# Loading the index first, broadcasting coefficients by a matmul, halving the first parts, and adding W to one block by DMA

## The chip, the cores and the metric

The kernel runs on one core of a Trainium2 chip. TensorE multiplies matrices into PSUM; VectorE and ScalarE work element by element; GpSimd and SyncE here mostly issue DMAs. SyncE, ScalarE and GpSimd each have a DMA queue of their own, and all queues share the core's 16 DMA engines. The metric is the device time of one execution in microseconds (us), lower is better: 408.46 us is the median of three runs before the change.

## What is computed

Two layers follow each other on x, eight batches of 256 tokens by 1024. In the first layer each batch has its own integer mask of 1024 by 1024 and its own coefficient; in the second each batch picks one of eight weight matrices by an index.

```python
def _L0_cond_ref(hidden_states, W, b, coeff, mask):
    output = jnp.einsum('bsi,oi->bso', hidden_states, W) + b
    sign = (2 * mask - 1).astype(hidden_states.dtype)
    diff = jnp.einsum('bsi,bio->bso', hidden_states, sign)
    return output + diff * coeff[:, None, None]

def _L1_cond_ref(x, weight, adapter_ids):
    w = weight[adapter_ids]
    return jnp.einsum('bsi,boi->bso', x, w)

x = x + _L0_cond_ref(x, L0_cond_W, L0_cond_b, condB_coeff, mask_Bx4096x4096_ik1)
x = x + _L1_cond_ref(x, L1_cond_weight, itok_B_3_7)
```

For one batch the first layer is one product: x times (W transposed + coeff * (2 * mask - 1)). So each mask block is scaled on ScalarE to 2 * coeff * mask - coeff and W is added to it ("folded") before it is used as a weight.

## The kernel before

**Stages.** The very first stage is batch 0 of layer 0 (L285 on TensorE): eight row blocks k of mask and W, 128 rows each, are loaded in nine pieces, scaled on ScalarE (L271), folded on VectorE (L278) and multiplied. All other stages are pairs of a layer and a batch, in the order (1,0), (0,1), (0,2), (1,1), (0,3), (1,2) and so on up to (1,7). In this text they are stage 1, stage 2, stage 3 and so on; stage 1 uses L553 on TensorE, the later ones L563. The third batch (b = 2) of layer 0 is stage 3.

**A stage.** Each matrix of 1024 by 1024 is cut into four blocks "11", "12", "22", "21" of 512 by 512 (1 MB each, 8 KB in each of 128 partitions). Seven block products, p1 to p7 in the manner of Strassen and Winograd, stand for eight: p1, p5, p6, p2, p7, p3, p4 in this order on TensorE. The sums of weight blocks t1 to t4 (L515) and of input blocks s1 to s4 (L503) are made on VectorE, the products are added to the result on VectorE (L627), and two of them are copied out of PSUM by ScalarE on the way (L599: s after p1, u after p6; p7 waits for u, since it continues in the same PSUM bank). In layer 0, ScalarE scales each mask block (L476) and VectorE folds W into it (L490). The sum t1 is block 12 minus block 11; p5 needs s1 and t1, p1 needs block 11 itself, and s1 is a21 + a22.

**Results and residuals.** The residual of a batch is loaded by SyncE (L370), and the bias is added to it by a DMA with addition on GpSimd's queue (L380). Results of layer 0 are transposed on VectorE (L400) and moved into place by 32 small ScalarE operations (L414), which the first product of layer 1 for this batch waits for. Finished blocks are stored by GpSimd's queue (L653), 256 KB each, 2 KB in each partition.

**What sets the order.** Every engine has its own queue and works through it in order. The order is made when the kernel is built: each operation is a task with an engine, a length and a due time; plan() runs through them with a list of ready tasks for each engine, takes the most urgent one whose buffers are free, and the instructions are written in the order of the planned starts. Weight blocks live in eleven buffers ("w"). Changed lengths, or a task on another engine, can therefore reorder all that follows. At most eight loads are under way at once: SyncE issues a load only when the one eight places before it has landed.

**Around the change.** The coefficients come as a DMA that repeats one row in 128 partitions (L742); two VectorE operations make 2c and -c of it (L751, L752). The index of the second layer's weights (ids_sb, L756) and the bias column b_sb (L757) are issued on SyncE's queue when the last but two of the first stage's folds has been written down. SyncE reads the index into a register (L470) before the first weight load of stage 1 (L472); this read waits until the index has landed. Four evictions (L312) turn the first stage's PSUM banks into the input of stage 1. Eight matmuls on zeros (L750) run at the start.

Of the kernel before, what the change touches and what calls it, by code (L numbers as in the profile page):

```python
# [17 lines left out]
WBUFS = 11  # L18


PRODUCTS = (
    ("p1", "a11", "11"),
    ("p5", "s1", "t1"),
    ("p6", "s2", "t2"),
    ("p2", "a12", "21"),
    ("p7", "s3", "t3"),
    ("p3", "s4", "22"),
    ("p4", "a22", "t4"),
)

BANK = {"p1": "u", "p6": "u", "p7": "u", "p4": "u", "p5": "v", "p3": "v", "p2": "w"}
A_SLOT = {"a11": 0, "a12": 1, "a21": 2, "a22": 3, "s1": 4, "s2": 5, "s3": 2, "s4": 6}
# [9 lines left out]
}  # L42


PRODUCT, BLOCK, SMALL = 3.44, 2.30, 0.72
SCALE, COPY, SHUFFLE = 2.12, 0.65, 0.47
LOAD, STORE, LATENCY = 2.55, 0.65, 2.2


class Task:  # L50
# [20 lines left out]
def plan(tasks, room, may_take):  # L71
# [11 lines left out]
    for t in tasks:  # L83
        ready.setdefault(t.engine, [])
        if not waiting[t]:
            ready[t.engine].append(t)
    free_at = dict.fromkeys(ready, 0.0)
    left = {}
    events, now, done = [], 0.0, 0
    while done < len(tasks):  # L90
        for engine, queue in ready.items():
            if free_at[engine] > now + 1e-9:
# [34 lines left out]
def kernel(  # L127
# [58 lines left out]
    const = pools["const"]  # L186
    ids_sb = const.tile([1, B], I32, name="ids_sb")
    b_sb = const.tile([P, KC], F32, name="b_sb")
    c_sb = const.tile([P, B], F32, name="c_sb")
    c2_sb = const.tile([P, B], F32, name="c2_sb")  # L190
    cn_sb = const.tile([P, B], F32, name="cn_sb")
    warm = const.tile([P, 1], F32, name="warm")
    zeros = const.tile([P, H], BF16, name="zeros")
    w0_sb = const.tile([P, KC, 2, H], F32, name="w0_sb")
# [1 line left out]

    def block(q: str) -> int:
        return 2 * (int(q[0]) - 1) + int(q[1]) - 1

    w1_blocks = w1T.rearrange("n q p k o -> (n q) p k o")  # L200
    tasks: list[Task] = []
# [2 lines left out]
    def task(*args, **kw):  # L204
        tasks.append(Task(*args, **kw))
        return tasks[-1]
# [35 lines left out]
    first = {(j, h): Buffer("ps") for j in range(2) for h in range(2)}  # L242
    xb = Buffer("r")
    half = KH // 2
    pieces = [(0, ds(0, H)), (0, ds(H, H))] + [(k, ds(0, D)) for k in range(1, KC)]
    w0_rows = w0_sb.rearrange("p k j n -> p k (j n)")

    def x0_view():
# [7 lines left out]
    def load_x0(lo: int, hi: int, queue):  # L256
        queue.dma_start(out=x0_view()[:, lo:hi], in_=x0T[:, lo:hi])

    def load_first(n: int):
        k, cols = pieces[n]  # L260
        if m[k // 2].tile is None:
            take(m[k // 2])
        nc.sync.dma_start(out=m_view(k)[:, cols].bitcast(I32), in_=mask0[k][:, cols])  # L263
        nc.sync.dma_start(out=w0_rows[:, k, cols], in_=w0T[k][:, cols])  # L264
        if n in (1, 2, 4):
            load_x0(*{1: (1, 2), 2: (2, KH), 4: (KH, KC)}[n], nc.sync)

    def scale_first(n: int):
        k, cols = pieces[n]
        t = m_view(k)[:, cols]  # L270
        nc.scalar.activation(  # L271
            t, t.bitcast(I32), AF.Identity, bias=cn_sb[:, 0:1], scale=c2_sb[:, 0:1]
        )

    def fold_first(n: int):
        k, cols = pieces[n]
        t = m_view(k)[:, cols]
        v.tensor_tensor(t, t, w0_rows[:, k, cols], ALU.add)  # L278

    def mm_first(k: int, cols):  # L280
        for oc in range(cols.start // P, (cols.start + cols.size) // P):
# [35 lines left out]
        )  # L317

    at = 2.0
    folded: list[Task] = []  # L320
    for n, (k, cols) in enumerate(pieces):
        share = cols.size / D
        ld = task(
            "DMA",
            2.7 * share,
            lambda n=n: load_first(n),
            takes=[m[k // 2]] if n == 0 or (k % 2 == 0 and n > 1) else [],
            uses=[] if n == 0 or (k % 2 == 0 and n > 1) else [m[k // 2]],
            latency=2.0,
            latest=0.1 * n,  # L330
        )
        sc = task("ACT", 1.25 * share, lambda n=n: scale_first(n), after=[ld], uses=[m[k // 2]])
        fo = task("DVE", 1.25 * share, lambda n=n: fold_first(n), after=[sc], uses=[m[k // 2]])
        folded.append(fo)
        last_scale = sc
        if n == 0:
            tasks[0].takes = [x0] + list(tasks[0].takes)
            tasks[0].uses = [x0] + list(tasks[0].uses)
            x0.users += 1
# [90 lines left out]
    def stage(s: int):  # L430
# [49 lines left out]
        for q in BLOCKS:  # L480
            W[q] = Buffer("w")
            t = task("DMA", LOAD, lambda q=q: load(q), takes=[W[q]], latency=LATENCY)
            t.stage = s
            loads.append(t)
            if layer == 0:
                t = task("ACT", SCALE, lambda q=q: scale(q), after=[t], uses=[W[q]])
                t = task(
                    "DVE",
                    BLOCK,
                    lambda q=q: v.tensor_tensor(W[q].tile, W[q].tile, w0[q], ALU.add),  # L490
                    after=[t],
                    uses=[W[q]],
                )
            done[q] = t
        ready_r = load_r(b, begin) if layer == 0 else None

        def sum_of(what: str, after=()):
            left, op, right = SUMS[what]
            if what[0] == "s":
                done[what] = task(  # L500
                    "DVE",
                    SMALL,
                    lambda: v.tensor_tensor(part(what), part(left), part(right), op),  # L503
                    after=[*got, done.get(left), done.get(right), *after],
                    takes=[apart] if flipped and what == "s3" else [],
                    uses=[A],
                )
                return
            src = [W[left], W[right]]
            fresh = what in ("t2", "t3") or (what == "t1" and s == 1)  # L510
            W[what] = Buffer("w") if fresh else W[left]

            def emit():
                a, c = src[0].tile, src[1].tile
                v.tensor_tensor(take(W[what]) if fresh else W[what].tile, a, c, op)  # L515

            t = task(
                "DVE",
                BLOCK,
                emit,  # L520
                after=[done[left], done[right], *after],
                takes=[W[what]] if fresh else [],
                uses=src,
            )
            if fresh:
                t.stage = s
            done[what] = t

        sum_of("s1")
        sum_of("s2")  # L530
# [38 lines left out]
                    skip_group_check=True,  # L569
                )  # L570

        def add_product(n: int, after=()):
            nonlocal last_mm
            name, a, w = PRODUCTS[n]
            bank = BANK[name]
            opens = bank not in banks
            if opens:
                banks[bank] = Buffer("ps")
            r = banks[bank]
            needed = got if a[0] == "a" else []  # L580
            if flipped and a == "a11":
                needed = got[:2]
            mm[name] = last_mm = task(
                "PE",
                PRODUCT,
                lambda: product(name, a, w, r, opens),
                after=[last_mm, done[w], done.get(a), *needed, *after],
                takes=[r] if opens else [],
                uses=[A, W[w]] + ([] if opens else [r]) + ([apart] if flipped and a == "s3" else []),
                latest=begin + n * PRODUCT,  # L590
            )

        def keep(name: str, source: str):
# [65 lines left out]
                latency=3.0,  # L659
            )  # L660

        add_product(0)
        s1, s1_done = keep("s1", "p1")
        add_product(1)
        add("11", s1, ALU.add, s1_done)
        add_product(2, [s1_done])
        t = add("22", banks["v"], ALU.add, mm["p5"])
        u2, u2_done = keep("u2", "p6")
        add("12", u2, ALU.add, u2_done)
        add_product(3)  # L670
        sum_of("t4", [mm["p2"]])
        add("11", banks["w"], ALU.add, mm["p2"])
        finished("11")
        add_product(4, [u2_done])
        add_product(5, [t])
        t = add("22", banks["u"], ALU.add, mm["p7"])
        finished("22")
        if final:
            t = add("21", banks["u"], ALU.add, mm["p7"])
        add("12", banks["v"], ALU.add, mm["p3"])  # L680
        finished("12")
        if not final:
            add_product(6, [t])
            add("21", banks["u"], ALU.add, mm["p4"])
            finished("21")
        else:
# [52 lines left out]

    with tc.manual_schedule():  # L740
        take(x0)
        nc.scalar.dma_start(out=c_sb, in_=coeff.to_broadcast((P, B)))  # L742
        load_x0(0, 1, nc.scalar)
        v.memset(zeros, 0.0)
        v.memset(warm, 0.0)  # L745

        nc.scalar.activation(warm, warm, AF.Identity, bias=warm, scale=1.0)
        idle = pools["ps"].tile([P, H], F32, tag="ps", name="idle")
        for _ in range(8):
            nc.tensor.matmul(out=idle, lhsT=zeros[:, 0:P], rhs=zeros, start=True, stop=True)  # L750
        v.tensor_scalar(c2_sb, c_sb, 2.0, None, ALU.mult)  # L751
        v.tensor_scalar(cn_sb, c_sb, -1.0, None, ALU.mult)  # L752
        for n, t in enumerate(plan(tasks, room, may_take)):
            t.emit()
            if t is folded[-3]:
                nc.sync.dma_start(out=ids_sb, in_=ids)  # L756
                nc.sync.dma_start(out=b_sb, in_=biasT)  # L757
    if DUMP:
        for t in sorted(tasks, key=lambda t: t.start):
            print("PLAN %s %.2f %.2f %.2f" % (t.engine, t.start, t.end, t.latest))  # L760
# [55 lines left out]
```

## Time and profile before

| What | Value |
|---|---|
| Median of three runs | 408.46 us (408.2 to 408.93) |
| The profiled execution: its time, its span | 408.25 us, 406.5 us |
| Granted TensorE clock | 0.999 |
| ScalarE busy | 183.1 us (45%) |
| GpSimd busy | 25.9 us (6%) |
| HBM traffic | 94.38 MB read, 8.39 MB written |
| Fold of W into a 1 MB mask block on VectorE (L490) | 28 of 2281 ns |
| Sum of two weight blocks on VectorE (L515) | 60 of 2285 ns |
| Scaling of a 1 MB mask block on ScalarE (L476) | 28 of 2091 ns |
| Bias addition by DMA (L380), issue to landing | 7 of 7.8 to 16.4 us, median 9.9 |
| Store of a finished block (L653), issue to landing | 31 of 2.0 to 17.8 us, median 6.2 |

The span runs from the first to the last instruction in one profiled execution. "Busy" counts instructions on an engine; TensorE's matmuls are pipelined and each is recorded as two records in this program. A "wait" line names who waited, who ended the wait, and the time in total, how often, and the longest.

### The profile page before, as it was taken

The page shows a single profiled execution, that of the slowest core. Times are in us where ns is not written, and L with a number is a line of the kernel's source. Part 1 is how long each engine was busy: PE and PEld are TensorE (multiplying, and loading weights), DVE is VectorE, ACT ScalarE, POOL GpSimd, SP SyncE. Part 2 cuts the span into 40 slices and gives each one's busy share as a digit, 9 for nine tenths or more (in the row PEclk, how much of TensorE's full clock was granted, in tenths as well). Part 3 has the DMA queues.
Part 4 walks back from the last instruction along what each step waited for, and adds up shares of the span by engine and source line. Part 5 has one row for each costly group of instructions (what it writes and reads, how often), then busy time and mean ns, then how long its engine had stood idle before and what let it go on. Part 6 is the DMA issues. An engine that isn't in the chain of part 4 may idle for free.

```text
span 406.5 us, 3436 instructions
## 1 busy us (share of the span) xinstructions
PE 395.7 (97%) x1152; PEld 201.2 (49%) x1152; DVE 329.5 (81%) x300; ACT 183.1 (45%) x301; POOL 25.9 (6%) x42
## 2 busy tenths in 40 slices
PE   6997999999999999999999999999999999999996
PEld 3886996443444444444444444444444444444443
DVE  1345989899999979989989999799997989878142
ACT  4351642221991079422867445495117940283000
POOL 0000022001000210011100101002010010001101
PEclk9999999999999999999999999999999999999999
DMA  7979999998863869928697457987569582611102
GB/s 267 411 290 426 423 392 336 348 388 344 231 272 113 304 212 256 410 94 329 215 376 285 147 187 225 343 339 243 214 154 406 230 303 104 268 42 52 52 0 104
DMA packets 18804, 103.00 MB, mean 253 GB/s; under 512 B 2466, under 2 KB 2978, under 8 KB 9314
## 3 DMA queue, kind: packets, MB, share of 16 engines
q1 hardware_dynamic: 13970, 87.11, 54.7%
q0 software_dynamic: 4384, 15.47, 15.0%
q10 hardware_dynamic: 432, 0.20, 0.2%
q8 instruction: 9, 0.15, 0.1%
q14 instruction: 9, 0.07, 0.1%
HBM read 94.38 MB, written 8.39 MB: 253 GB/s over the span
## 4 chain that ended last, share of the span: by engine, by line
PE 82%; DMA 8%; DVE 4%; ACT 3%; issue 1%; SPq 1%; DVEq 0%; ACTq 0%
PE ps L563 77%; PE ps L553 5%; DMA w<-mask 4%; ACT a L414 3%; DMA ids_sb<-ids 2%; DMA w<-w1T 2%; DVE w L515 2%; DVE w L490 1%; DVE a L312 1%; DVE a L503 0%; DVE r L627 0%; SPq L264 0%; SPq L263 0%; SPq L470 0%; ACT u L599 0%
## 5 line engine op out<-in xcount | busy, mean ns | idle before, releaser
L563 PE MATMUL ps<-w,a 128*128 128x512 f32 (+1 forms) x792 | 337.2, 588 | 1.2 <-DVE a L503 0.7
L563 PEld LDWEIGHTS ps<-w,a 128*128 128x128 f32 x792 | 149.7, 190 | 188.6 <-issue 181.8
L515 DVE TENSOR_TENSOR w<-w,w 128x2048 f32<-128x2048 f32 x60 | 136.4, 2285 | 10.8 <-DMA w<-w1T 5.5
L414 ACT ACTIVATE a<-turn 32x256 f32<-32x256 f32 x224 | 92.7, 414 | 32.1 <-DVE turn L400 29.4
L476 ACT ACTIVATE w<-w,cn_sb,c_sb 128x2048 f32<-128x2048 int32 x28 | 58.2, 2091 | 32.6 <-DMA w<-mask 32.3
L627 DVE TENSOR_TENSOR r<-r,ps 128x512 f32<-128x512 f32 x73 | 49.5, 682 | 22.3 <-PE ps L563 21.6
L490 DVE TENSOR_TENSOR w<-w,w_sb 128x2048 f32<-128x2048 f32 x28 | 63.7, 2281 | 3.2 <-ACT w L476 3.2
L599 ACT ACTIVATE s<-ps 128x512 f32<-128x512 f32 x15 | 8.9, 594 | 85.4 <-PE ps L563 85.4
L503 DVE TENSOR_TENSOR a<-a 128x512 f32<-128x512 f32 x59 | 39.2, 680 | 0.1
L653 POOL DMA_DIRECT2D out<-r x31 | 17.5, 565 | 242.3 <-DVE r L627 239.4
L285 PE MATMUL ps<-a,w 128*128 128x256 f32 x128 | 29.4, 394 | 2.0 <-DVE w L278 2.0
L285 PEld LDWEIGHTS ps<-a,w 128*128 128x128 f32 x128 | 25.3, 199 | 6.6 <-DVE w L278 2.9
L599 ACT ACTIVATE u<-ps 128x512 f32<-128x512 f32 x15 | 9.0, 597 | 39.9 <-PE ps L563 39.2
L553 PE MATMUL ps<-a,w 128*128 128x128 f32 x192 | 22.3, 277 | 2.9 <-DVE a L312 2.2
L553 PEld LDWEIGHTS ps<-a,w 128*128 128x128 f32 x192 | 21.7, 192 | 3.6 <-DVE a L312 2.6
L278 DVE TENSOR_TENSOR w<-w,w_sb 128x1024 f32<-128x1024 f32 (+1 forms) x9 | 10.0, 1106 | 14.9 <-DMA w_sb<-w0T 9.4
L400 DVE STREAM_TRANSPOSE turn<-r 128x512 f32<-128x512 f32 x28 | 18.9, 695 | 0.1
L380 POOL DMA_DIRECT2D r<-bias x7 | 8.7, 1247 | 132.6 <-DMA r<-xR 132.6
L271 ACT ACTIVATE w<-w,cn_sb,c_sb 128x1024 f32<-128x1024 int32 (+1 forms) x9 | 10.3, 1145 | 15.1 <-DMA w<-mask 13.2
L627 DVE TENSOR_TENSOR r<-r,s 128x512 f32<-128x512 f32 x14 | 9.5, 681 | 8.1 <-ACT s L599 8.0
L627 DVE TENSOR_TENSOR r<-r,u 128x512 f32<-128x512 f32 x14 | 9.6, 688 | 6.8 <-ACT u L599 6.7
L750 PE MATMUL idle<-zeros 128*128 128x512 bf16 x8 | 3.6, 631 | 1.2 <-DVE warm L745 1.2
(20 smaller groups left out, 21.2 us busy)
## 6 DMA issues: line engine op xcount, KB each, us to landing
w<-w1T SPq DMA_DIRECT2D x32, 1024.0 KB, 6.9
w<-mask SPq DMA_DIRECT2D x28, 1024.0 KB, 9.5
out<-r POOLq DMA_DIRECT2D x31, 256.0 KB, 6.4
a<-xT SPq DMA_DIRECT2D x7, 1024.0 KB, 10.8
r<-xR SPq DMA_DIRECT2D x7, 1024.0 KB, 7.3
r<-bias POOLq DMA_DIRECT2D x7, 1024.0 KB, 9.9
w<-mask SPq DMA_DIRECT2D x7, 512.0 KB, 10.2
w_sb<-w0T SPq DMA_DIRECT2D x7, 512.0 KB, 9.6
```

Of the source, the lines that this page charges most:

```text
L285: nc.tensor.matmul(out=t.rearrange("p (c n) -> p c n", c=half)[:, c % half], lhsT=m_view(k)[:, ts(oc, P)], rhs=x0_view()[:, k], start=k == ...
L400: lambda t=t, opens=not turned: v.transpose(out=(take(r) if opens else r.tile)[:, t], in_=view(source.tile)[:, 2 * t + j]),
L414: nc.scalar.activation(to[:, :, :, f], src[:, :, :, g], AF.Copy)
L476: nc.scalar.activation(t, t.bitcast(I32), AF.Identity, bias=cn_sb[:, b : b + 1], scale=c2_sb[:, b : b + 1])
L490: lambda q=q: v.tensor_tensor(W[q].tile, W[q].tile, w0[q], ALU.add),
L503: lambda: v.tensor_tensor(part(what), part(left), part(right), op),
L515: v.tensor_tensor(take(W[what]) if fresh else W[what].tile, a, c, op)
L553: nc.tensor.matmul(out=t[:, ts(c, TH)], lhsT=W[w].tile[:, k, ts(c, P)], rhs=part(a)[:, k], start=opens and c == 0 and k == 0, stop=k == KH ...
L563: nc.tensor.matmul(out=t[:, cols], lhsT=part(a)[:, k], rhs=W[w].tile[:, k, cols], start=opens and k == 0, stop=k == KH - 1, skip_group_che ...
L599: lambda: nc.scalar.activation(take(r), bank.tile, AF.Copy),
L627: v.tensor_tensor(to, left, get(r), op)
L653: lambda: (queue or nc.gpsimd).dma_start(out=out0[:, block(q)] if flipped else out[b - 1, :, int(q[0]) - 1, lo:hi], in_=R[b].tile[:, block ...
```

## The change

1. The coefficients are loaded as one row, and a matmul with a row of ones spreads them over 128 partitions in PSUM; VectorE reads them there. There are nine matmuls on zeros instead of eight, and the new one stands after the fifth.
2. The index is loaded at the start on ScalarE's queue. So is the first part of W; the first part of x goes to SyncE's queue. The bias column is issued by ScalarE with piece 4.
3. The row blocks k = 0 and k = 1 are loaded in halves, and the very first half is scaled and folded in two steps. Mask and W of a piece are now two tasks of the plan.
4. In stage 1 the sum t1 is made in two halves.
5. For the block (2, "11"), which is block 11 of the third batch, W is added by a DMA with addition on GpSimd's queue after the scaling, instead of by VectorE.
6. The plan's lengths are a little shorter and its DMA starts at 1.7. The list of products is rewritten as a table and an order, with the same products in the same order.

```diff
-PRODUCTS = (
-    ("p1", "a11", "11"),
...
+BY_DMA = ((2, "11"),)
+ORDER = ("p1", "p5", "p6", "p2", "p7", "p3")
...
-PRODUCT, BLOCK, SMALL = 3.44, 2.30, 0.72
-SCALE, COPY, SHUFFLE = 2.12, 0.65, 0.47
-LOAD, STORE, LATENCY = 2.55, 0.65, 2.2
+PRODUCT, BLOCK, SMALL = 3.435, 2.29, 0.69
+SCALE, COPY, SHUFFLE = 2.10, 0.60, 0.42
+LOAD, STORE, LATENCY, BEGIN = 2.50, 0.60, 2.2, 1.7
...
+    free_at["DMA"] = BEGIN
...
-    c_sb = const.tile([P, B], F32, name="c_sb")
+    c_row = const.tile([1, B], F32, name="c_row")
+    ones = const.tile([1, P], F32, name="ones")
...
+    def w0_block(q: str):
+        i, j = int(q[0]) - 1, int(q[1]) - 1
+        return w0T[ts(i, KH), :, ts(j, H)].rearrange("k p n -> p k n")
...
-    pieces = [(0, ds(0, H)), (0, ds(H, H))] + [(k, ds(0, D)) for k in range(1, KC)]
+    pieces = [(k, ds(j * H, H)) for k in range(2) for j in range(2)]
+    pieces += [(k, ds(0, D)) for k in range(2, KC)]
...
-    def load_first(n: int):
+    def load_mask(n: int):
         k, cols = pieces[n]
         if m[k // 2].tile is None:
             take(m[k // 2])
         nc.sync.dma_start(out=m_view(k)[:, cols].bitcast(I32), in_=mask0[k][:, cols])
-        nc.sync.dma_start(out=w0_rows[:, k, cols], in_=w0T[k][:, cols])
-        if n in (1, 2, 4):
-            load_x0(*{1: (1, 2), 2: (2, KH), 4: (KH, KC)}[n], nc.sync)
+        if n == 0:
+            load_x0(0, 1, nc.sync)
+
+    def load_w0(n: int):
+        k, cols = pieces[n]
+        if n:
+            nc.sync.dma_start(out=w0_rows[:, k, cols], in_=w0T[k][:, cols])
+        if n in (1, 3, 5):
+            load_x0(*{1: (1, 2), 3: (2, KH), 5: (KH, KC)}[n], nc.sync)
+        if n == 4:
+            nc.scalar.dma_start(out=b_sb, in_=biasT)
+
+    def parts(n: int):
+        k, cols = pieces[n]
+        if n:
+            return k, [cols]
+        return k, [ds(cols.start, cols.size // 2), ds(cols.start + cols.size // 2, cols.size // 2)]
...
-                t = task(
-                    "DVE",
-                    BLOCK,
-                    lambda q=q: v.tensor_tensor(W[q].tile, W[q].tile, w0[q], ALU.add),
-                    after=[t],
-                    uses=[W[q]],
-                )
+                if (b, q) in BY_DMA:
+                    t = task(
+                        "POOL",
+                        1.3,
+                        lambda q=q: nc.gpsimd.dma_start(
+                            out=W[q].tile, in_=w0_block(q), accum_op=ALU.add
+                        ),
+                        after=[t],
+                        uses=[W[q]],
+                        latency=9.0,
+                    )
+                else:
+                    t = task(
+                        "DVE",
+                        BLOCK,
+                        lambda q=q: v.tensor_tensor(W[q].tile, W[q].tile, w0[q], ALU.add),
+                        after=[t],
+                        uses=[W[q]],
+                    )
...
+            parts = (slice(0, KH),)
+            if s == 1 and what == "t1":
+                parts = (slice(0, KH // 2), slice(KH // 2, KH))
...
-        nc.scalar.dma_start(out=c_sb, in_=coeff.to_broadcast((P, B)))
-        load_x0(0, 1, nc.scalar)
+        nc.scalar.dma_start(out=c_row, in_=coeff)
+        nc.scalar.dma_start(out=w0_rows[:, 0, pieces[0][1]], in_=w0T[0][:, pieces[0][1]])
+        nc.scalar.dma_start(out=ids_sb, in_=ids)
         v.memset(zeros, 0.0)
+        v.memset(ones, 1.0)
...
-        for _ in range(8):
+        c_ps = pools["ps"].tile([P, B], F32, tag="ps", name="c_ps")
+        for n in range(9):
             nc.tensor.matmul(out=idle, lhsT=zeros[:, 0:P], rhs=zeros, start=True, stop=True)
-        v.tensor_scalar(c2_sb, c_sb, 2.0, None, ALU.mult)
-        v.tensor_scalar(cn_sb, c_sb, -1.0, None, ALU.mult)
-        for n, t in enumerate(plan(tasks, room, may_take)):
+            if n == 4:
+                nc.tensor.matmul(out=c_ps, lhsT=ones, rhs=c_row, start=True, stop=True)
+                v.tensor_scalar(c2_sb, c_ps, 2.0, None, ALU.mult)
+                v.tensor_scalar(cn_sb, c_ps, -1.0, None, ALU.mult)
+        for t in plan(tasks, room, may_take):
             t.emit()
-            if t is folded[-3]:
-                nc.sync.dma_start(out=ids_sb, in_=ids)
-                nc.sync.dma_start(out=b_sb, in_=biasT)
```

## The prediction

> **What bounds the kernel now.** I read the busy times first, then who TensorE waited for, then the chain of waits, then the DMA load by stretch.
>
> ```profile
> PE 395.7 (97%) x1152; PEld 201.2 (49%) x1152; DVE 329.5 (81%) x300; ACT 183.1 (45%) x301; POOL 25.9 (6%) x42
> ...
> PE ps L553 <- DVE a L312: 2.2, 1, 2.2
> PE ps L285 <- DVE w L278: 2.0, 1, 2.0
> PE ps L553 <- DVE a L503: 0.7, 1, 0.7
> PE ps L563 <- DVE a L503: 0.7, 1, 0.7
> PE ps L563 <- ACT a L414: 0.5, 1, 0.5
> ```
>
> TensorE is busy 97% of the span, so only its gaps and its slow start can be won. They are few: 2.0 us before the first stage, 2.2 and 0.7 around the start of stage 1, 0.7 in stage 3 and 0.5 before stage 4. The chain of waits places them:
>
> ```profile
> 18.68 8.21 DMA ids_sb<-ids
> ...
> 28.44 6.90 DMA w<-w1T
> ...
> 92.23 0.61 DVE a L503
> ...
> 92.98 7.12 PE ps L563 x16
> ...
> 100.18 0.60 ACT u L599
> ...
> 114.32 288.72 PE ps L563 x680
> ```
>
> From 114.32 us on TensorE runs without a gap, 288.72 us for 680 records, 0.4246 us each. All that can be gained lies before that time. The index is issued at 18.68 and lands at 26.89; SyncE waits for it, so the first weight load of stage 1 is issued only at 27.89. The DMA engines run empty meanwhile. (Columns: stretch, its length, busy PE, PEld, DVE, ACT, POOL, clock, DMA share, GB/s.)
>
> ```profile
> 26.00:27.00 1.00, 1.00 (x7) 0.87 (x6) 0.38 (x1) 0.00 (x0) 0.00 (x0) 1.00 0.67 233
> 27.00:28.00 1.00, 1.00 (x6) 0.90 (x5) 0.00 (x0) 0.60 (x1) 0.00 (x0) 1.00 0.07 25
> 28.00:29.00 1.00, 1.00 (x6) 0.87 (x5) 0.27 (x1) 0.83 (x2) 0.00 (x0) 1.00 0.48 70
> 29.00:30.00 1.00, 1.00 (x7) 0.87 (x6) 0.95 (x1) 1.00 (x3) 0.00 (x0) 1.00 0.37 115
> ...
> 59.00:69.00 10.00, 10.00 (x64) 7.61 (x63) 9.96 (x7) 4.79 (x3) 0.76 (x2) 1.00 1.04 305
> 69.00:75.00 6.00, 6.00 (x16) 2.65 (x15) 5.32 (x7) 2.10 (x1) 1.84 (x2) 1.00 1.03 421
> 75.00:85.00 10.00, 10.00 (x25) 4.50 (x24) 8.68 (x7) 2.69 (x2) 0.00 (x0) 1.00 1.03 310
> ```
>
> The lost DMA time is 0.33 + 0.93 + 0.52 + 0.63 = 2.4 us. From 30 to 95 us the DMA engines are full. Where the bias is added by DMA (59 to 69, 75 to 85) they move 305 to 310 GB/s, where they only copy 421: an addition is dear, and the change adds one.
>
> **Index, coefficients, first parts.** (a) *Index at once.* The load moves to ScalarE's queue at the start and SyncE's wait goes. The four weight loads now follow the first stage's loads directly, so the whole stream comes 2.4 us earlier. Block 12 lands at 35.34 - 2.4 = 32.9. Nothing of value stands behind the moved issue: ScalarE issues three small DMAs in place of two before its table load (one more at about 0.4 us), and is ready at about 3.8, before the first mask part (0.75 + 3.9 = 4.65).
>
> (b) *Coefficients.* The broadcast load of 128 rows landed at 4.86, and the first scaling began at 5.16, 0.5 us after its mask part. One row, and a matmul of eight columns after five idle matmuls (1.2 + 5 x 0.43 = 3.4 us), end that. A one-row load is not in the trace; the 64 KB store at the end lands in 2.0 us, the broadcast in 4.1: between 2.8 and 4.9, I take 3.4, which costs nothing.
>
> (c) *Smaller first parts.* The last fold of row block k=1 ended at 11.65, that of k=2 at 14.85. From k=1 on TensorE never waited, 36.17 - 11.65 = 24.5 us for seven blocks, 3.50 each; so k=1 set the end. With halves, k=1's first half is folded about 10 and its second at 11.0 (w0 lands 10.32 + 0.69), and k=2, whose bytes come no sooner, sets it: 14.85 + 6 x 3.50 = 35.83, 0.34 us earlier. Bounds: 0 to 0.8 (if k=2 came 0.5 sooner). The two extra ScalarE and VectorE instructions lie in idle time (1.3 to 2.6 us before each later one).
>
> The first eight records took 3.25 us (0.41 each) where later ones take 0.22. The Trainium skill, "TensorE: Matmul & The Clock Gate", section "What's actually happening", says the array runs at half rate until some 3.4 us of sustained work; the ninth idle matmul would then save up to 16 x 0.19 = 3 us by the page, and by the sum above nothing, as data of k=2 sets the end either way.
>
> (d) *Order on VectorE.* Before, the sum t1 (L515) stood ahead of the evictions (L312) and waited 5.5 us for block 12, until 35.43; stage 1 began at 38.38. In the built order of the changed kernel two evictions stand first, then t1 in halves, then the other two. Half 0 of TensorE's first stage ends 3.5 us before 35.83, so: evictions 32.4 to 33.7, t1 33.7 to 36.1, evictions to 37.4, s1 to 38.0. The first product needs two evictions and can follow at once, at 35.9. It takes 3.99; the second starts at 39.9 instead of 43.10. **Minus 3.2 us**, made of 0.3 + 2.2 + 0.7. The price if the cover is gone: t1's data would have to be 1.9 us later than 32.9 before TensorE noticed.
>
> **The addition by DMA.** (e) It takes one 2.28 us block (L490) off VectorE just before t3 and t1 of stage 3. There t1 ended at 91.5 and s1 at 92.8, and TensorE waited for s1: 64 records from 64.65 to 92.98 took 28.33 against 27.17 at 0.4246, 1.16 lost. 3.2 us earlier and 2.28 less work, t1 ends at 86.0 and s1 at 87.2, and the product is due at 88.6: **minus 1.16**, if W has arrived. VectorE reaches t1 at 83.8; TensorE reaches the first product of that stage, which reads the block itself, at 85.2.
>
> (f) *When it arrives.* The mask block landed 18.0 after its issue at 41.15, 59.1; now 56.7, scaled by 58.8, then issued by GpSimd for about 1.3 us. On GpSimd's DMA queue stand, ahead of it, the first bias addition (54.5 + 16.0 = landed 70.4) and two stores (72.2 and 74.5). Behind: a store (76.3, so 1.8 us) and the second bias addition (69.6 + 16.4 = 86.0, so 9.75 us after the store). W is as large as a bias addition, and I take 9.75: 74.5 + 9.75 - 2.4 = **81.8**. Slack 2.0 us to VectorE's t1 (3.3 counted to where TensorE would notice), 3.4 to TensorE.
>
> (g) *Who is pushed back.* The store lands at 83.7, the second bias addition at **93.4**. VectorE's first add of stage 3 needs that bias. By its order it gets there at 92.8 (s1 87.2, t2, an add, s2, a fold of 2.2), and behind it stand the transposes for ScalarE's chain of 32 moves (L414, 13.6 us), which releases stage 4. That chain starts when the copy before it ends, 100.7 - 4.4 = 96.3; two transposes and the add take 1.9. So the bias may land at 94.3: 0.9 us of slack. Plain loads are slowed by some 3 us per addition ((423 - 305)/423 x 10); those of stage 4 landed at 86.7 to 93.9 and were used from 103.7. SyncE's load of the next residual waits for the stores and comes some 6 us later in the kernel's own time; it is used in stage 5, from about 137. The bias column for the first stage (b_sb) goes to ScalarE's queue between two scalings, 0.4 us in an idle stretch of 1.3 or more. The rewritten list of products emits the same products in the same order.
>
> The 0.5 us before stage 4 stays, as ScalarE's chain moves with TensorE. Sum: 3.2 + 1.2 = 4.4. The profiled execution took 408.25 us around its span of 406.5; span 402.1. The median is 0.2 above that execution: 408.46 - 4.4 = **404.1 us**.
>
> The Trainium skill, "SBUF — State Buffer", section "A bandwidth-pool intuition that's wrong (but worth ruling out)", speaks against this: a GpSimd DMA beside a VectorE copy took 3,100 ns instead of 620, as it waited for its descriptors. VectorE is full of two-operand sums here, yet the bias issues show 1.19 to 1.37 us. By the page, as an estimate, the issue would last five times 1.25, some 6 us, and end at 65, still before the store at 72 lands: no change of the sum.
>
> **Rivals.** The price of W's pieces is the open point. Its rows are 2 KB where the bias has 4 KB. The stores have 2 KB rows too, and the queue's 4384 packets for 15.47 MB are, less 16 end marks for each of 38 transfers, 4.1 KB each: rows are packed in pairs. That speaks for 9.75.
>
> *Slower: addition paid per row.* If each 2 KB row costs what 4 KB cost, W takes 19.5: lands 91.6, the bias 103.2, 8.9 late at VectorE's add, and transposes, moves and stage 4 with it. 8.9 - 4.4 = +4.5: 413 us. It decides from 15 us on (9.75 + 0.9 + 4.4). For it: no addition of 2 KB rows is in the trace. Against: the packing.
>
> *No change: rows go singly, at half price.* A bias addition is 16 rounds per engine of 0.61, 0.31 of it the copy between (1.05 MB alone, 2.47 us, eight rounds). 32 rounds of 0.31 + 0.15 are 14.7: bias at 98.4, 4.1 late, 408.2.
>
> *Head only.* W or the bias is late by 1 to 3 us because the queue starts later than I think (the first addition's first packets took some 4 us): 405.2 to 407.
>
> *Head covered.* If the stream does not move (first-stage loads lag), block 12 lands at 35.3 as before; evictions first still save 2.2: about 406.
>
> **Chances.** Forecast 0.58; head only or covered 0.13; no change 0.10; slower 0.19. About 0.2% (0.8 us) is what can be told from no change. Faster 0.71, same 0.10, slower 0.19. The forecast's own range is 403.0 to 405.2 (part c's bounds, 1 us of late bias); 8 in 10 needs 403.0 to 409.2.
>
> **What would show it.** Right: stage 1 follows the first stage within 0.3 us and its second product starts near 39.9; DMA share stays near 1 from 5 to 90 us; W lands near 82 and takes about 10; no TensorE wait near 88; stage 4 starts near 109.9. Wrong: VectorE idle before t1 or before the first add of stage 3 with a DMA as releaser, or a new gap after 110.

## The result, and the profile after

| | Median | Ratio to before, with its 95% interval |
|---|---|---|
| Before | 408.54 us (408.09 to 409.65) | |
| Changed kernel | 408.75 us (407.95 to 409.84) | 1.0002 [0.9993, 1.0011] |

The time did not change, where 404.1 us was forecast. The profiled execution of the changed kernel took 409.84 us, the longest of its twelve and 1.1 us above their median; its span is 408.1 us.

The waits of TensorE in the profile after (who waited, who ended it: us in total, times, longest):

```profile
PE ps L310 <- DVE w L303: 3.1, 2, 1.7
PE ps L613 <- ACT a L446: 1.8, 1, 1.8
...
PE ps L613 <- DVE a L547: 0.9, 1, 0.9
PE ps L613 <- PE ps L613: 0.5, 1, 0.5
```

L310 is now the first stage, L603 stage 1, L613 the later ones. The wait of 2.2 us for the evictions at the start of stage 1 is gone. In its place stand waits in the middle of the first stage, two in stage 3 and one of 1.8 us before stage 4. The chain of waits after (start, length, what) says where:

```profile
8.43 8.21 DMA w_sb<-w0T
16.74 1.24 DVE w L303
18.02 20.99 PE ps L310 x96
39.00 25.01 PE ps L603 x224
64.02 24.05 PE ps L613 x56
88.06 0.52 issue
88.58 10.76 PE ps L613 x24
99.37 0.61 ACT u L649
99.97 0.47 issue
100.44 0.35 DVE r L677
...
101.05 1.31 DVE turn L432 x2
...
116.05 288.72 PE ps L613 x680
```

Read it from the end. From stage 4 on the same 288.72 us follow as before, but stage 4 starts at 116.05, not at 114.32 as before and not at 109.9 as forecast. Ahead of it stand the 32 moves of ScalarE, the transposes, and an addition of VectorE that starts at 100.44. At the front, stage 1 follows the first stage at once, as forecast, but at 39.00 (forecast 35.83, before 38.38): the first stage waited for W's part of row block k=2, which landed at 16.64 and not at 13.54. So there are two losses. VectorE's timeline after shows the second (start, length, instruction, idle before it and who ended it):

```profile
88.59 2.29 DVE L564 TENSOR_TENSOR w<-w,w 128x2048 f32<-128x2048 f32 x1 [1.30 <-DMA w<-w0T]
...
100.44 0.69 DVE L677 TENSOR_TENSOR r<-r,s 128x512 f32<-128x512 f32 x1 [2.76 <-ACT u L649]
```

VectorE waits for the W addition itself before t1, and then 2.76 us at the add that needs the second bias addition. The profile names ScalarE there, but its copy had ended at 99.97; the bias landed at 100.36, and it is the DMA that ended the wait. W was issued at 61.50, the store before it landed at 74.16, W at 88.50, the store behind it at 90.61, the bias at 100.36. So W took 14.3 us from the landing of the store before it, where 9.75 was forecast. The packets of GpSimd's queue rose from 4384 to 4912: 512 more of 2 KB, and 16 end marks (small packets that close a transfer). The rows of W went singly.

The stretches after (stretch, length, busy PE, PEld, DVE, ACT, POOL, clock, DMA share, GB/s) show the first loss, and what became of the index:

```profile
9.00:10.00 1.00, 1.00 (x4) 0.73 (x4) 0.11 (x1) 0.81 (x1) 0.00 (x0) 1.00 0.67 182
10.00:11.00 1.00, 1.00 (x4) 0.82 (x3) 0.59 (x1) 0.69 (x1) 0.00 (x0) 1.00 0.66 96
11.00:12.00 1.00, 1.00 (x6) 0.89 (x5) 0.69 (x1) 0.13 (x1) 0.00 (x0) 1.00 0.77 170
...
27.00:28.00 1.00, 1.00 (x6) 0.90 (x5) 0.00 (x0) 1.00 (x1) 0.00 (x0) 1.00 1.07 430
```

From 27 to 28 us, where 25 GB/s were moved before, there are now 430: the hole of the index (the stretch in which next to nothing was moved) is closed. But from 9 to 12 us there is a new one, 96 to 182 GB/s where the kernel before moved 408 to 424 in the same stretch. The packets in it are long: packets of 2 KB took 118 to 210 ns in the mean, single ones up to 705, against 84 ns before.

### The profile page after: what moved, and what is told of

It is laid out like the page before. It is cut to its first block, busy times and chain, and to the rows that moved or that the text cites. A ratio compares the mean times of both kernels' runs of the same rounds, so it can differ in the third digit from the quotient of the medians.

```text
span 408.1 us, 3449 instructions
## 1 busy us (share of the span) xinstructions
PE 397.2 (97%) x1155; PEld 201.7 (49%) x1155; DVE 328.0 (80%) x303; ACT 183.9 (45%) x303; POOL 27.3 (7%) x43
## 3 DMA queue, kind: packets, MB, share of 16 engines
q0 software_dynamic: 4912, 16.52, 15.6%
## 4 chain that ended last, share of the span: by engine, by line
PE 91%; ACT 3%; DMA 3%; DVE 1%; issue 1%; SPq 0%; ACTq 0%; DVEq 0%
PE ps L613 79%; PE ps L603 6%; PE ps L310 5%; DMA w_sb<-w0T 3%; ACT a L446 3%; DVE turn L432 0%; DVE w L303 0%; SPq L272 0%; ACT u L649 0%; ACTq L801 0%; SPq L279 0%; SPq L266 0%; DVE r L677 0%; DVE r L761 0%; DVEq L303 0%
## 5 line engine op out<-in xcount | busy, mean ns | idle before, releaser
L613 PE MATMUL ps<-w,a 128*128 128x512 f32 (+1 forms) x792 | 337.6, 588 | 3.3 <-ACT a L446 1.8
L613 PEld LDWEIGHTS ps<-w,a 128*128 128x128 f32 x792 | 149.6, 190 | 191.3 <-issue 184.0
L564 DVE TENSOR_TENSOR w<-w,w 128x2048 f32<-128x2048 f32 (+1 forms) x61 | 136.8, 2249 | 6.7 <-PE ps L613 4.4
L534 DVE TENSOR_TENSOR w<-w,w_sb 128x2048 f32<-128x2048 f32 x27 | 61.5, 2278 | 2.9 <-ACT w L508 2.9
L310 PE MATMUL ps<-a,w 128*128 128x256 f32 x128 | 30.0, 398 | 3.1 <-DVE w L303 3.1
L310 PEld LDWEIGHTS ps<-a,w 128*128 128x128 f32 x128 | 25.5, 201 | 8.1 <-DVE w L303 4.4
L303 DVE TENSOR_TENSOR w<-w,w_sb 128x1024 f32<-128x1024 f32 (+2 forms) x11 | 10.2, 934 | 18.5 <-DMA w_sb<-w0T 14.0
L603 PE MATMUL ps<-a,w 128*128 128x128 f32 x192 | 21.8, 275 | 0.0
L603 PEld LDWEIGHTS ps<-a,w 128*128 128x128 f32 x192 | 21.7, 192 | 0.1
L295 ACT ACTIVATE w<-w,cn_sb,c_sb 128x1024 f32<-128x1024 int32 (+2 forms) x11 | 11.0, 1006 | 17.1 <-DMA w<-mask 16.3
```

The costliest lines, as they stand in the source:

```text
L310: nc.tensor.matmul(out=t.rearrange("p (c n) -> p c n", c=half)[:, c % half], lhsT=m_view(k)[:, ts(oc, P)], rhs=x0_view()[:, k], start=k == ...
L564: v.tensor_tensor(to[:, rows], a, c, op)
L603: nc.tensor.matmul(out=t[:, ts(c, TH)], lhsT=W[w].tile[:, k, ts(c, P)], rhs=part(a)[:, k], start=opens and c == 0 and k == 0, stop=k == KH ...
L613: nc.tensor.matmul(out=t[:, cols], lhsT=part(a)[:, k], rhs=W[w].tile[:, k, cols], start=opens and k == 0, stop=k == KH - 1, skip_group_che ...
```

## The experiments

Theory A: the rows of 2 KB make the W addition late, and the second bias addition and stage 4 with it. Theory B: the gain is lost in the first stage. Each ratio is to the kernel before in the same group of runs.

**e1, the changed kernel without the addition.** VectorE folds W into all blocks.

```diff
-BY_DMA = ((2, "11"),)
+BY_DMA = ()
```

> The changed kernel with W of all blocks added by VectorE (nothing added by DMA); the rest of the change stays. Theory A (the addition by DMA takes 15.7 us, lands late and pushes the second bias addition from 86.0 to 100.4, so stage 4 starts at 116.0): without it the bias lands near 86 again, TensorE waits about 1.2 us for s1 in stage 3 as before the change, and stage 4 starts near 113.5 (114.3 less the 0.8 us that stage 2 starts earlier): ratio to the kernel before about 0.998. Theory B (the loss lies in the first stage alone, the addition does what it should): without it TensorE waits 1.2 us more than in the changed kernel, ratio about 1.003.

406.99 us, ratio 0.9966 [0.9946, 0.9986]: without the addition the kernel is faster than with it. That speaks for A. The hole near 10 us was there too (115 GB/s), stage 1 began at 40.65 in the chain. Five of its twelve executions, the profiled one among them, had a granted clock of 0.992 to 0.996 and took 408.24 to 409.84 us, the other seven 406.21 to 407.32; what such a clock means is shown in the last section.

**e2, the kernel before with the addition alone.**

```diff
+BY_DMA = ((2, "11"),)
...
+                if (b, q) in BY_DMA:
+                    t = task(
+                        "POOL",
+                        1.3,
+                        lambda q=q: nc.gpsimd.dma_start(
+                            out=W[q].tile, in_=w0_block(q), accum_op=ALU.add
+                        ),
...
```

> The kernel before with nothing changed but the addition by DMA for block 11 of the third batch. Theory A: W lands near 90 (74.5 + 15.7), 2 us after the first product of stage 3 wants it (88.4), the second bias addition lands near 102 instead of 86, VectorE's first add of stage 3 waits for it until then instead of 99.6, and stage 4 starts near 117.6 instead of 114.3: ratio about 1.008. Theory B: the wait of 1.2 us for s1 goes and nothing else changes: ratio about 0.997.

407.99 us, ratio 0.9981 [0.9972, 0.999]: a miss of theory A. W landed at 89.34, the bias at 101.21, as late as in the changed kernel, and yet nothing was lost. The reason is in the built order, which the new task changed (chain of waits of e2):

```profile
95.72 0.60 DVE a L520
96.32 0.62 DVE turn L405
96.94 2.17 DVE w L507
99.12 0.63 DVE turn L405
...
103.60 0.49 ACT u L616
104.08 0.04 issue
104.13 15.95 PE ps L580 x36
```

Here two transposes (L405) and the first moves of ScalarE stand ahead of the copy u and of the add that needs the bias. In the changed kernel all 32 moves stand behind that add. A late bias is paid only where the order puts the chain behind it.

**e3, the changed kernel with W added in rows of 8 KB.** A second copy of W lies in memory in the layout of the blocks; only the addition reads it.

```diff
-        return w0T[ts(i, KH), :, ts(j, H)].rearrange("k p n -> p k n")
+        return w0B[2 * i + j]
...
+        "w0B": blocks(np.asarray(L0_cond_W).T),
```

> The changed kernel with a second copy of W in memory, laid out block by block, from which alone the addition by DMA reads: 8 KB in a row for each partition instead of four rows of 2 KB. The amount added is the same. Theory A (the price is one of rows: 2 KB pieces take turns one by one with the 8 KB pieces of the loads): pieces of 4 KB or more, the addition takes about 10 us, W lands near 83, the bias near 94.5, stage 4 starts near 112 to 113: ratio about 0.995 to 0.997. Rival (the price is one of the amount added, whatever the rows): about 15 us as in the changed kernel, ratio 1.000.

405.25 us, ratio 0.9925 [0.9899, 0.995]. W landed 7.4 us after the store before it (72.86 to 80.23), the bias at 92.36, no wait in stage 3. Theory A holds; the hole near 10 us stayed (156 GB/s, stage 1 at 37.91), so B holds too, for a smaller part.

**e4, the kernel before with the index load moved to the start of ScalarE's queue.**

```diff
         load_x0(0, 1, nc.scalar)
+        nc.scalar.dma_start(out=ids_sb, in_=ids)
...
-                nc.sync.dma_start(out=ids_sb, in_=ids)
```

> The kernel before with nothing changed but the index load, issued on ScalarE's queue at the start. If the early index is worth what was predicted, the DMA engines stay full from 26 to 30 us, block 12 lands near 33 instead of 35.3, VectorE's sum t1 starts there, and stage 1 starts at once after the first stage (36.2) instead of 38.4: 2.2 us, ratio about 0.995. If the head's gain is a matter of the whole stream and lost again before stage 4 (ScalarE's chain of moves), the ratio is 1.000 with stage 4 at 114.3.

407.21 us, ratio 0.996 [0.9947, 0.9972]. The index alone gains 1.6 us, less than the 2.4 us of empty DMA time: k=2 landed at 14.56 instead of 13.54, and the stretches of e4 show a hole at the same place, which the kernel before does not have:

```profile
9.00:10.00 1.00, 1.00 (x4) 0.82 (x3) 0.09 (x1) 0.82 (x1) 0.00 (x0) 1.00 0.92 211
10.00:11.00 1.00, 1.00 (x6) 0.85 (x6) 1.00 (x1) 0.00 (x0) 0.00 (x0) 1.00 0.79 176
```

So four more runs asked what brings the hole, all on top of e3: C, the early index load; D, W's first part on ScalarE's queue, for whose landing SyncE's later loads wait (issued at 3.57, the next only at 6.22); E, the 2 KB rows of row block k=1.

**e5, index load behind the bias column.**

```diff
             nc.scalar.dma_start(out=b_sb, in_=biasT)
+            nc.scalar.dma_start(out=ids_sb, in_=ids)
...
-        nc.scalar.dma_start(out=ids_sb, in_=ids)
```

> The e3 kernel (W added in 8 KB rows) with one move: the index load leaves the start of ScalarE's queue and goes behind the bias column, about 10 us in. In e3 the DMA engines moved only 156 and 205 GB/s between 10 and 12 us, W's part of row block k=2 landed at 15.55 instead of 13.54 and stage 1 began at 37.75. Theory C, the early index load brings the slow packets: over 380 GB/s from 7 to 15 us, k=2 lands near 13.6, stage 1 begins near 35.8 to 36.2, ratio to before 0.9925 - 1.7/408.5 = 0.988. Theories D (W's first part on ScalarE's queue) and E (k=1 in 2 KB rows): the dip stays, k=2 near 15.5, ratio 0.9925 within 0.0015.

405.17 us, ratio 0.9921 [0.9907, 0.9934]. The profile agrees with C: 317 to 365 GB/s from 9 to 11 us, k=2 at 14.14, no wait for k=2. The time does not: it is that of e3. The profiled execution took 404.01 us; of the five others one took 404.03 and four 405.15 to 406.04. Whether those four had the hole, the one profile cannot show.

**e6, x's first block and W's first part changed over, as before.**

```diff
-        if n == 0:
-            load_x0(0, 1, nc.sync)
...
-        if n:
-            nc.sync.dma_start(out=w0_rows[:, k, cols], in_=w0T[k][:, cols])
+        nc.sync.dma_start(out=w0_rows[:, k, cols], in_=w0T[k][:, cols])
...
-        nc.scalar.dma_start(out=w0_rows[:, 0, pieces[0][1]], in_=w0T[0][:, pieces[0][1]])
+        load_x0(0, 1, nc.scalar)
```

> The e3 kernel with the first loads of x and of W changed over as in the kernel before: x's first block on ScalarE's queue, W's first part on SyncE's; index early as in e3. Theory D, the first W part on ScalarE's queue holds back SyncE's loads and so brings the dip: SyncE issues its ninth load near 4.8 instead of 6.22, k=2 lands near 13.6, stage 1 near 36, ratio 0.988. Theories C and E: the dip near 10 us stays, k=2 at 15 or later, ratio 0.9925 within 0.0015.

404.65 us, ratio 0.991 [0.9897, 0.9923]. The hole stayed (139 GB/s from 10 to 11), so D does not bring it; but SyncE's load after the one at 3.57 goes out at 5.51 instead of 6.22, and all that follows is 0.7 us earlier (k=2 at 14.86).

**e7, k=1 loaded in whole rows, scaled and folded in halves.**

```diff
-        nc.sync.dma_start(out=m_view(k)[:, cols].bitcast(I32), in_=mask0[k][:, cols])
+        if k == 1:
+            cols = ds(0, D)
+        if n != 3:
+            nc.sync.dma_start(out=m_view(k)[:, cols].bitcast(I32), in_=mask0[k][:, cols])
...
-        if n:
+        if k == 1:
+            cols = ds(0, D)
+        if n not in (0, 3):
             nc.sync.dma_start(out=w0_rows[:, k, cols], in_=w0T[k][:, cols])
```

> The e3 kernel with row block k=1 loaded in whole rows of 4 KB (one load of the mask, one of W), scaled and folded in halves as in e3. Theory E, the 2 KB rows of k=1 bring the slow packets: no dip near 10 us, k=2 lands near 13.6, stage 1 near 36, ratio 0.988. Theories C and D: the dip stays, k=2 at 15 or later, ratio 0.9925 or, as the first half of k=1 comes later, up to 0.994.

404.35 us, ratio 0.9905 [0.9891, 0.9919]. No hole at 9 to 12 (406 to 430 GB/s), although the index is early: k=2 at 13.85, stage 1 at 36.90. This speaks for E, but in e4 the hole came with whole rows. Neither C nor E alone is the rule.

**e8, the moves of e5 and e6 together.**

> The e3 kernel with both moves: the index load behind the bias column, and x's first block and W's first part changed over as in the kernel before. If C or D holds, each with its own part: k=2 lands near 13.6, stage 1 near 35.8, stage 2 near 61, stage 4 near 109.5, ratio 0.987 to 0.989 (403.5 us). If E alone holds: as e3, ratio 0.9925 within 0.0015.

403.80 us, ratio 0.989 [0.9875, 0.9904]: the time that was forecast (404.1), though by a kernel with a second copy of W and other first loads. Its stretches near 10 us and its chain of waits:

```profile
9.00:10.00 1.00, 1.00 (x5) 0.84 (x4) 0.66 (x1) 0.54 (x1) 0.00 (x0) 1.00 1.07 399
10.00:11.00 1.00, 1.00 (x7) 0.87 (x6) 0.69 (x1) 0.28 (x1) 0.00 (x0) 1.00 1.04 414
```

```profile
5.86 29.84 PE ps L309 x128
35.71 25.01 PE ps L602 x224
60.72 34.35 PE ps L612 x80
...
95.09 0.60 ACT u L648
...
109.23 288.72 PE ps L612 x680
```

TensorE runs from 5.86 us on without a wait until the 0.4 us before stage 4.

**e9, the changed kernel with the two moves of e8, W in its 2 KB rows.** The addition reads W as the change has it; the rest is e8.

> The changed kernel with the two moves of e8 alone (index behind the bias column; x's first block and W's first part changed over); W is added in its 2 KB rows, as the change has it. Theory A, the 2 KB rows are what takes the gain away: from e8's store at 71.3, W lands 14.3 later at 85.6 (14.3 as in the changed kernel), the store 2.1 later, the second bias addition 9.8 after that at 97.5, and stage 4 15.7 us after the bias, as in the changed kernel, at 113.2: 4 us later than e8's 109.23, ratio 0.989 + 4.0/408.4 = 0.9985. Rival, the loss lay in the head and the rows are hidden once it is gone: ratio 0.989 within 0.0015.

407.12 us, ratio 0.9961 [0.9949, 0.9974]. The chain of waits of e9:

```profile
36.49 25.01 PE ps L601 x224
61.50 24.05 PE ps L611 x56
85.80 10.76 PE ps L611 x24
...
113.27 288.72 PE ps L611 x680
```

W landed at 85.71, the bias at 97.58, stage 4 began at 113.27, each within about 0.1 us of what theory A said. The ratio is 0.0024 (1 us) better than the 0.9985 that was worked out from e8's (and 0.989 + 4.0/408.4 is rather 0.9988). Most of that gap has a plain reason: the 109.23 stands in e8's profiled execution, which took 403.00 us, 0.8 us less than the median to which e8's ratio belongs.

**e10, e8 with W in rows of 4 KB.** The second copy of W is laid out in rows of that length.

```diff
-                            out=W[q].tile, in_=w0_block(q), accum_op=ALU.add
+                            out=W[q].tile.rearrange("p (t k) n -> p t (k n)", t=2),
+                            in_=w0_block(q),
+                            accum_op=ALU.add,
```

> The e8 kernel with W added in 4 KB rows, the bias's size, in place of 8 KB. If an addition of 1 MB in 4 KB rows takes what the bias takes: W lands 9.75 after the store before it, at 81.1, the bias at about 92.9, VectorE's add that needs it was due at 92.66 in e8: ratio 0.989 to 0.9905. If anything below 8 KB goes like 2 KB: W at 85.6, bias 97.5, ratio 0.9985.

403.84 us, ratio 0.9882 [0.9863, 0.9901]. W took 10.2 us (71.19 to 81.41), the bias landed at 92.85, in time:

```profile
36.08 25.01 PE ps L604 x224
61.09 34.35 PE ps L614 x80
...
109.60 288.72 PE ps L614 x680
```

Where e9 stops in stage 3, TensorE runs on here, and stage 4 begins 3.7 us earlier; 0.4 of them were there already at stage 1. By the medians of the same group the longer rows are worth 3.3 us. One reservation: e9 reads W itself and e10 the copy; a copy in rows of 2 KB was not run.

**e11, e8 without the addition.** The edit is that of e1.

> The e8 kernel without the addition by DMA: VectorE adds W to all blocks of the third batch. What the addition is worth when its rows are long: VectorE has one block of 2.28 us more before s1 of stage 3, TensorE waits there for 0.7 to 1.2 us as before: stage 4 near 110.2, ratio 0.991 to 0.992. If the addition is worth nothing even so: ratio 0.989 within 0.001.

404.64 us, ratio 0.99 [0.9883, 0.9917]. The waits of TensorE in e11:

```profile
PE ps L612 <- DVE a L546: 1.1, 1, 1.1
PE ps L612 <- ACT a L445: 0.4, 1, 0.4
```

The wait of 1.1 us for s1 in stage 3 is back. So the addition, where it lands in time, is worth 0.8 us by the medians against e10; the intervals of the two ratios overlap, but this wait stands in all four profiles without the addition (before, e1, e4, e11) and in none of the seven in which it has rows of 4 or 8 KB.

**e12, the e3 kernel again.**

> The e3 kernel a second time, for the slow packets near 10 us: the profile of e3 had them, those of the runs with a late index load had none. If they belong to the kernel: DMA rate under 250 GB/s somewhere between 9 and 12 us again, k=2 at 15 or later, ratio 0.9925. If they fall by chance: in about half of such profiles none, k=2 near 13.6, stage 1 near 36.

405.59 us, ratio 0.9921 [0.9897, 0.9945]. The hole was there again (191 GB/s from 10 to 11), k=2 at 15.91: twice in the two profiles of this kernel.

## Why the prediction failed, step by step

Two terms were wrong. Step (f) gave W 9.75 us behind the store before it, and it took 14.3. And the arrival of k=2, which (a) and (c) took as unchanged, came 3.1 us later.

- **(a) Index at once.** The hole at 26 to 30 us closed, as said. But the stream did not come 2.4 us earlier: the first stage's loads had lost 3 us by then (the last of them landed at 31.67, before at 28.64), and the second weight load of stage 1, which t1 needs, came at 36.7, not at 32.9. In e8 it landed at 33.46. The step put the price of the early issue at nothing ("Nothing of value stands behind the moved issue"), and for the changeover of the first loads of W and x the prediction has no term at all; taking both back was worth 1.7 us (e9). The rival "head covered" had named such a lag, without a cause for it.
- **(b) Coefficients.** They came at no cost, as said: the first scaling began at 4.35, before at 5.16.
- **(c) Smaller first parts.** This step failed. It took the arrival of k=2 as given ("whose bytes come no sooner") and let it come no later either; 0 to 0.8 us of gain were its bounds. k=2 landed 3.1 us later and the first stage ended at 39.00, not 35.83. Where the loads come in time the sum holds: in e8 the fold of k=2 ended at 14.66, the 96 records from there on take 20.99 us, and the stage ended at 35.71. But that k=1 set the end before is not what the trace of before shows:

```profile
6.75 29.42 PE L285 MATMUL ps<-a,w 128*128 128x256 f32 x128 [1.96 <-DVE w L278]
```

TensorE ran the 128 records in one piece and waited for no later row block; with its slow first records it came to k=1 at 11.84, 0.2 us after that fold. (The clock column reads 1.00 in that stretch all the same; the slowness is seen in the records' own times, 0.41 us each against 0.22.) The slow start, which was weighed with the Trainium skill's page "TensorE: Matmul & The Clock Gate", decided nothing afterwards, as said: in the changed kernel the first 32 records took 9.05 us (in e3 7.17), and TensorE still waited 1.74 us for k=2.
- **(d) Order on VectorE.** This step was right: stage 1 follows the first stage at once in every run with this order.
- **(e) One block off VectorE.** This step was right in kind: it is worth 0.8 us by the medians (e10 against e11), where 1.16 was said. In the changed kernel it could not show, since W was not there.
- **(f) When W arrives.** This step failed: 9.75 us rested on "rows are packed in pairs", read from the stores' packets, which go from SBUF to memory. The addition reads rows of 2 KB in memory, and each went as its own packet: 14.3 us. The trace of before had a sign of it: the loads of 2 KB rows from memory on SyncE's queue went in 640 packets of 2 KB. The rival "rows go singly, at half price" had 14.7 us, the right mechanism. That its 408.2 us came so near the measured 408.75 is in part luck: it had the bias at 98.4, not at 100.36, and no loss in the first stage. For rows of 4 KB the sum was right to 0.5 us (e10: 10.2).
- **(g) Who is pushed back.** The chain was right to the end, but its slack of 0.9 us was used up by (c) and (f). The store ahead of W landed 2.1 us later than the sum's 72.1, W took 4.6 more, the store behind it 0.2: bias at 100.36 instead of 93.4. Less the slack that is 6.1, and stage 4 began 6.15 us after the forecast's 109.9. GpSimd's issue of the addition took 1.33 us beside a busy VectorE. The estimate of 6 us from the Trainium skill's "SBUF — State Buffer", section "A bandwidth-pool intuition that's wrong (but worth ruling out)", did not come true here.

So by the ratios: the rows cost 0.0079 (e9 to e10, 3.2 us), the order of the first loads 0.0041 (the changed kernel to e9, 1.7 us; these two stand in different groups of runs, and their profiles differ by 2.5 us at the start of stage 1). Together these are 4.9 us, more than the 4.4 that were forecast.

## What to carry to other kernels

Count the packets of a DMA that reads from memory by its rows there and not by its bytes: rows of 2, 4 and 8 KB went in packets of 2, 4 and 8 KB here. Do not take the count over from stores, whose rows of 2 KB went in packets of 4 KB; why they do, no run here shows. Then price the packets with the packets of the other queue that go between them. Where a gain rests on loads that come early, look at every load that is moved ahead of them, small ones too. And before pricing a late transfer, look at what the built order puts behind it: e2 paid nothing for the same lateness.

## What the runs showed of the hardware

**Queues take turns packet by packet.** While W was added, the two busy queues sent:

| Rows of W | Its packets, ns each | From its first packet to its last | SyncE's packets of 8 KB in that time | From the landing of the store before it to its own |
|---|---|---|---|---|
| 2 KB (e9) | 512, 176 | 15.2 us | 494 | 14.2 us |
| 4 KB (e10) | 256, 327 | 10.6 us | about 270 | 10.2 us |
| 8 KB (e8) | 128, 628 | 8.5 us | 159 | 7.4 us |

One packet of SyncE's (some 320 ns) goes for about each packet of the addition. On 16 engines that is 32 x (0.176 + 0.32) = 15.9 us, 16 x (0.327 + 0.32) = 10.4 and 8 x (0.628 + 0.32) = 7.6 us, each within 1 us of the third column. The addition's own packets took 5.0 to 5.6 us in all three; the rest is SyncE's turn. The Trainium skill, "DMA: Bandwidth & Descriptors", section "Queues, rings and completion order", says that each engine goes round between its queues packet by packet; these counts agree with it. With that rule and packets of one row each, the price could have been worked out: the rival's 14.7 us is such a sum.

**After a wait TensorE can run at half clock for 3.4 us.** In e12 it waited 3.11 us for k=2, in e3 2.94. The two timelines of TensorE, e12 first, and then the stretches of e12 (busy PE, PEld, DVE, ACT, POOL, clock, DMA share, GB/s):

```profile
17.29 22.67 PE L311 MATMUL ps<-a,w 128*128 128x256 f32 x96 [3.11 <-DVE w L304]
```

```profile
16.92 20.99 PE L311 MATMUL ps<-a,w 128*128 128x256 f32 x96 [2.94 <-DVE w L304]
```

```profile
18.00:19.00 1.00, 1.00 (x5) 0.83 (x5) 0.39 (x1) 0.50 (x1) 0.00 (x0) 0.73 1.01 406
19.00:20.00 1.00, 1.00 (x4) 0.82 (x3) 0.84 (x1) 0.00 (x0) 0.00 (x0) 0.50 1.04 414
20.00:21.00 1.00, 1.00 (x3) 0.77 (x3) 0.00 (x0) 0.00 (x0) 0.00 (x0) 0.50 1.04 414
21.00:22.00 1.00, 1.00 (x4) 0.79 (x3) 0.00 (x0) 0.91 (x1) 0.00 (x0) 0.57 1.02 406
```

The same 96 records took 1.68 us more, at a granted clock of 0.50; e1, after a wait of 3.96 us, shows the same 22.67. So the wait of 3.11 us in e12 cost 4.8. But the length of the wait alone does not decide it. In e2 the clock fell after a shorter one, of 2.41 us ahead of the first records:

```profile
6.95 29.58 PE L290 MATMUL ps<-a,w 128*128 128x256 f32 x128 [2.41 <-DVE w L283]
```

```profile
7.00:8.00 1.00, 1.00 (x4) 0.86 (x5) 0.25 (x1) 0.72 (x1) 0.00 (x0) 0.78 1.02 392
8.00:9.00 1.00, 1.00 (x4) 0.81 (x3) 0.45 (x1) 0.00 (x0) 0.00 (x0) 0.50 1.03 422
9.00:10.00 1.00, 1.00 (x4) 0.72 (x4) 0.00 (x0) 0.81 (x1) 0.00 (x0) 0.50 1.00 401
10.00:11.00 1.00, 1.00 (x4) 0.81 (x3) 0.45 (x1) 0.43 (x1) 0.00 (x0) 0.51 1.06 426
```

Both falls were equally long: the rows lose 0.27 + 0.50 + 0.50 + 0.43 = 1.70 us of clock in e12 and 0.22 + 0.50 + 0.50 + 0.49 = 1.71 in e2, which is 3.4 us at half clock. The Trainium skill, "TensorE: Matmul & The Clock Gate", section "What's actually happening", names an idle window of about 3.4 us after which the clock halves; here waits of 2.41 and 3.11 us were followed by it and one of 2.94 was not. What decides beside the length no run here was made to show.

One fall lowers the mean clock of an execution to 0.996 (1.7 of 407 us). Of the kernel before, 14 of 24, 2 of 11 and 5 of 13 executions in the three groups of runs had 0.996 or less, and its medians there were 408.93, 408.33 and 408.84 us. So ratios from different groups, those of e3 and e5 for one, can differ by 0.0015 through this alone.

**The hole near 10 us stays open.** In the seven profiles with the index load among the first loads it was there in six (the changed kernel, e1, e3, e4, e6, e12; not in e7), in the seven with a later one (before, e2, e5, e8 to e11) the rate never fell below 315 GB/s there (before, e2 and e8 kept 399 or more, e5 and e9 to e11 dipped to between 315 and 365). That is one profile for each kernel, and e5's other times warn that it need not stand for all. Why a load of 32 bytes should bring slow packets 7 us later no run here shows, and by the medians the index's move alone (e5 against e3) is not told from nothing; the changeover alone (e6 against e3) lies within the intervals too. Both together do tell (the changed kernel against e9).
